# Per-pass denominators by small DMAs instead of transposes, and both context halves transposed in one run

## The chip, the cores and the metric

The kernel runs on one core of a Trainium2 chip. The metric is the device time of one execution in microseconds (us), taken as the median of several executions. The profile is one further execution recorded by the hardware profiler; its own time stands beside the median below.

## The reference

Two graph layers run one after the other on `x` of shape 8 x 2048 x 256 with one adjacency matrix of 2048 x 2048. Layer 0 is a chunked attention with a softmax per chunk of 256 keys. Layer 1, the one that this change touches, is a graph attention with 4 heads of 64:

```python
h = relu(layernorm(x))                      # rows of 256
q = (h @ W).reshape(B, N, 4, 64)
e = e_src[:, :, None, :] + e_dst[:, None, :, :]
e = where(e >= 0, e, 0.2 * e)               # leaky relu
e = where(adj > 0, e, -9e15)
attn = softmax(e, axis=2)                   # over the 2048 sources j
x = x + elu(einsum('bijh,bjhd->bihd', attn, q).reshape(B, N, 256))
```

For each batch `b` and head `h` the kernel needs the weighted sums (the context, 64 numbers for each of 2048 rows) and the softmax denominators (one number for each row). It divides, applies elu, adds `x`, and stores 64 columns of the output.

## The kernel before

Layer 0 fills the first 2730 us or so and is not touched. The second layer is a list of 32 **passes**, one for each of 8 batches and 4 heads (`passes`, L887), of 16 **rounds** each (`rounds`, L888); round `jt` handles 128 sources `j` against all 2048 rows.

The main loop (L901 to L952) writes the instructions of each round by hand, in program order. Every engine takes its own instructions in that order, so an instruction that waits holds up all that stands behind it on its engine. In a round:

- VectorE (DVE) makes the weights `e` two rounds ahead (`clipped`, L804): a max of two factors, clipped by the adjacency limits. There are five `e` buffers, so the weights of round 10 go where those of round 5 were, and wait until every reader of those is done. At the pass's first round ScalarE (ACT) first writes the row factors `near` (L795).
- TensorE (PE) multiplies `e` with the values into two accumulator banks, one for each half of the 64 columns (`weigh_rows`, L815, 8 matmuls a round). Partition 32*blk + d holds column d of row block blk, and the free axis holds the 512 rows of the block.
- For the denominators the rounds go in pairs. ACT scales the even round's weights into two tiles `t` (L926), GpSimd (POOL) adds the odd round's weights to them (L932), and PE sums `t` over the partitions into the bank `den` two rounds later (`add_up_rows`, L826, 4 matmuls). So pair 2, rounds 4 and 5, is summed in round 7. Pairs 3 and 7 (`SINGLE`, L881) skip ACT and POOL and are summed round by round.
- After round 15 ACT copies the accumulators to `cT` (L939) and `den` to `dT` (L948). In `dT` the 512 denominators of block blk fill partition 32*blk and are repeated in the 31 below it.

What is left of a pass is done by a generator, `ending` (L838), during the first rounds of the next pass. `aside` (L194) is a list of generators. `advance` (L213) is called once a round (not in round 13), and resumes each of them once, in order, but stops after one that yields nothing (`None`); one that yields `True` lets the next go on. `ending` stands at the front (L949). Its steps are: load the residual columns `xh` (in round 15); transpose `dT` with four PE transposes and take reciprocals (round 0, yields `None`); transpose the first half of `cT` and multiply (round 1, `None`); the second half (round 2, `None`); then for each half of the rows four ACT operations (L870 to L873, rounds 3 and 5) and two POOL additions (L875, L876, rounds 4 and 6), yielding `True`; then the store (round 7).

Behind it stands `preparation(b + 1)` (L603), which makes the next batch's inputs during a batch's first passes: layer-norm factors on POOL (`roots`, L133 to L136), loads of `x1` (L111), normalisation on ACT (L145), transposes (L157) and copies (L165), small matmuls (L622), and at last eight projections of the values (`sides`, L154, with a DVE product, L693), one for each call of `advance`.

[...]four for `near`, two for the accumulators, and two in the tile `rest`: bank 0 is `den`, bank 1 is what `aux()` returns, used by all transposes and projections.

All loads of the second layer, but those of the first prepared batch, and the stores go through SyncE's queue (SP) in program order: `xh` (L842), the row factors' sources `es` (L594), `x1` (L111), the store (L878).

## Time and profile before

| | |
|---|---|
| median of 3 executions | 4205.73 us (4204.49 to 4206.44) |
| the profiled execution: its own time | 4210.55 us |
| its span, first to last instruction | 4208.7 us |
| granted TensorE clock, mean | 0.994 |
| first `dT` copy (end of pass 0) to the last (end of pass 31) | 2788.8 to 4191.2 us |
| L804, DVE, 128x2048 | 2343 ns, x448 |
| L932, POOL, 128x1024 | 2383 ns, x384 |
| L926, ACT, 128x1024 | 1142 ns, x384 |
| L858, DVE, 128x512 | 681 ns, x64 |
| L157 on `dT`, PE, 128x128 | 273 ns, x128 |

A row of the timeline gives the start, the duration, the engine, the line and operation, what it writes from what, and how many alike in a row; in brackets the idle time of the engine before it and what ended that. Successive instructions of one engine overlap a little [...], so starts are a better measure of pace than durations. Matmul records stand for several instructions on quarters of the array: a round of L815 takes 1.72 us from start to start, a sum of L826 0.86 us, four transposes 0.58 us.

### The profile page before, as it was taken

Reading aid. Unit: us, or ns where it says so; the run is one execution under the profiler, and the core shown is the slowest. Engines: PE = TensorE matmul, PEld = TensorE weight load, DVE = VectorE, ACT = ScalarE, POOL = GpSimd, SP = SyncE. Lnnn points to the kernel's source line nnn. Section 1 sums busy time; section 2 is a strip of 40 time slices with the busy share of each in tenths; the row PEclk is TensorE's granted clock in tenths of the full one; section 3 lists DMA queues with packets and bytes.
Section 4 is the critical chain, followed back from the end, with each engine's and each line's share of the span. In section 5 each row is a group of like instructions: output and inputs, shape, how many; then the busy total and the mean of one; then the engine's idle time right before and its main releaser. Section 6 shows DMA issues by size and latency. Waiting matters only on the chain. (4 is left out here: it accounts for less than half of the span.)

```text
span 4208.7 us, 85702 instructions
## 1 busy us (share of the span) xinstructions
PE 4067.2 (97%) x34998; PEld 1507.0 (36%) x34998; DVE 3159.1 (75%) x3526; ACT 2394.9 (57%) x3090; POOL 3263.0 (78%) x1735
## 2 busy tenths in 40 slices
PE   7999999999999999999999999889999999999998
PEld 3333333333333333333333333333333333333333
DVE  5786676666766677676677677588888988888897
ACT  5655565555565565555556556564555646555554
POOL 2577787888888888788788799777776877777687
PEclk9999999999999999999999999999999999999999
DMA  3221211112112112111211222221221222122121
GB/s 112 87 77 50 57 58 48 53 53 65 48 55 63 48 51 61 54 50 53 62 50 54 55 60 62 80 58 51 63 71 33 72 52 73 51 63 71 33 61 37
DMA packets 343235, 248.11 MB, mean 59 GB/s; under 512 B 225840, under 2 KB 293168, under 8 KB 342832
## 3 DMA queue, kind: packets, MB, share of 16 engines
q1 hardware_dynamic: 337648, 223.66, 19.6%
q0 software_dynamic: 5184, 18.88, 1.2%
q8 instruction: 277, 4.54, 0.4%
q14 instruction: 126, 1.03, 0.1%
HBM read 204.15 MB, written 36.18 MB: 57 GB/s over the span
## 5 line engine op out<-in xcount | busy, mean ns | idle before, releaser
L449 DVE SCALAR_TENSOR_TENSOR E<-big,limit 128x1024 f32<-128x1024 f32 x1024 | 1181.9, 1217 | 646.1 <-PE big L441 627.9
L742 POOL TENSOR_TENSOR add<-E 128x1024 f32<-128x1024 f32 x512 | 1203.7, 2374 | 496.1 <-PE both L461 472.7
L455 ACT ACTIVATE E<-E 128x1024 f32<-128x1024 f32 x1024 | 1055.7, 1057 | 687.8 <-DVE E L449 669.1
L804 DVE SCALAR_TENSOR_TENSOR e<-near,far,limit 128x2048 f32<-128x2048 f32 (+1 forms) x576 | 1183.0, 2107 | 94.3 <-issue 55.0
L932 POOL TENSOR_TENSOR t<-t,e 128x1024 f32<-128x1024 f32 x384 | 903.9, 2383 | 346.4 <-ACT t L926 196.0
L461 PE MATMUL both<-E,v 128*32 128x512 f32 x8192 | 993.9, 594 | 0.2
L815 PE MATMUL acc<-e,qn 128*32 128x512 f32 x8192 | 972.8, 595 | 5.3 <-DVE e L804 5.1
L441 PE MATMUL big<-qT,kT 64*128 64x512 f32 x4096 | 959.4, 606 | 14.6 <-DVE E L449 12.5
L441 PEld LDWEIGHTS big<-qT,kT 64*128 64x128 f32 x4096 | 366.2, 187 | 587.7 <-issue 419.8
L926 ACT ACTIVATE t<-e,quot 128x1024 f32<-128x1024 f32 x384 | 420.1, 1144 | 266.5 <-DVE e L804 153.1
L501 POOL TENSOR_TENSOR acc<-acc,c 128x1024 f32<-128x1024 f32 x224 | 531.2, 2371 | 4.6 <-DVE c L499 4.6
L461 PEld LDWEIGHTS both<-E,v 128*32 128x32 f32 x8192 | 294.3, 109 | 535.8 <-issue 396.7
L815 PEld LDWEIGHTS acc<-e,qn 128*32 128x32 f32 x8192 | 271.8, 110 | 496.0 <-issue 451.4
L499 DVE TENSOR_TENSOR c<-both,r 128x512 f32<-128x512 f32 x448 | 308.7, 690 | 42.3 <-PE both L461 10.6
L472 PE MATMUL big<-add,ones 128*32 128x512 f32 x2048 | 280.7, 601 | 13.9 <-POOL add L742 3.4
L826 PE MATMUL rest<-t,for_sums 128*32 128x512 f32 x1536 | 211.0, 594 | 22.2 <-DVE z L858 9.5
L479 ACT COPY s<-big 128x512 f32<-128x512 f32 x256 | 149.8, 585 | 71.1 <-PE big L472 70.8
L826 PE MATMUL rest<-e,for_sums 128*32 128x512 f32 x1024 | 141.0, 592 | 0.0
L145 ACT ACTIVATE h<-x,off,rstd 128x256 f32<-128x256 f32 x256 | 139.2, 593 | 0.0
L154 PE MATMUL rest<-w,hT 128*32 128x256 f32 x1952 | 122.1, 392 | 10.7 <-DVE qn L693 6.6
L795 ACT ACTIVATE near<-es,off_s 128x1024 f32<-128x1024 f32 x64 | 71.6, 1119 | 106.8 <-DVE e L804 95.8
L154 PE MATMUL big<-hT,wk 128*32 128x512 f32 x1024 | 124.2, 600 | 7.0 <-ACT hT L165 5.8
(133 smaller groups left out, 3031.3 us busy)
## 6 DMA issues: line engine op xcount, KB each, us to landing
r<-inv SPq DMA_DIRECT2D x1024, 64.0 KB
x<-in_x_dram SPq DMA_DIRECT2D x96, 512.0 KB
es<-er SPq DMA_DIRECT2D x64, 512.0 KB
adj_in<-in_adj_dram SPq DMA_DIRECT2D x32, 512.0 KB
x<-o POOLq DMA_DIRECT2D x32, 512.0 KB, 3.3
xh<-x SPq DMA_DIRECT2D x32, 512.0 KB
out_dram<-xh SPq DMA_DIRECT2D x32, 512.0 KB
x<-x SPq DMA_DIRECT2D x28, 512.0 KB
```

Of the source, the lines that this page charges most:

```text
L441: nc.tensor.matmul(ps[:, hh, :], ks[kt // NT][own, hp, (kt % NT) * P : (kt % NT + 1) * P], qs[qb][own, hp, :], start=True, stop=True,)
L449: nc.vector.scalar_tensor_tensor(e, ps, -0.5, bcast(limit[:, qb, kt, :], 1, 2), ALU.max, ALU.min)
L455: nc.scalar.activation(e, e, AF.Exp, scale=0.25 * EDGE)
L461: nc.tensor.matmul(both[part][32 * h : 32 * h + 32, :], vs[kt // NT][:, kt % NT, mine], es[h // 2][:, h % 2, :], start=first, stop=not first,)
L499: nc.vector.tensor_tensor(to[:, part, :], both[part], r, ALU.mult)
L501: nc.gpsimd.tensor_tensor(acc, acc, to, ALU.add)
L742: nc.gpsimd.tensor_tensor(both, tiles[0][hp], tiles[1][hp], ALU.add)
L804: nc.vector.scalar_tensor_tensor(e[:, of, :], near[:, of, :], far[:, jt, h : h + 1], limit[:, of, jt, :], ALU.max, ALU.min,)
L815: nc.tensor.matmul(acc[part][32 * blk : 32 * blk + 32, :], qn[jt // NT][:, jt % NT, own], e[:, blk, :], start=(jt == 0), stop=(jt == NKT - 1),
L826: nc.tensor.matmul(den[32 * blk : 32 * blk + 32, :], for_sums[:, jt, :], blocks[blk], start=first, stop=last,)
L926: nc.scalar.activation(t, now[:, 2 * half : 2 * half + 2, :], AF.Copy, scale=quot[:, m, h : h + 1])
L932: nc.gpsimd.tensor_tensor(ts[half], ts[half], now[:, 2 * half : 2 * half + 2, :], ALU.add)
```

## The change

`dT` is no longer transposed on PE. Four DMAs on SP's queue take the row of 512 denominators at partition 32*blk and lay it over 128 partitions, four numbers in each: partition p gets rows 4p to 4p + 3 of the block. The reciprocal then reads this tile in SBUF. So that the context comes out in the same arrangement, ACT writes `cT` with its columns reordered (it reads PSUM at steps of four), and `xh` and the output are moved by four DMAs each, a block at a time, with four neighbouring rows in a partition. Both halves of `cT` are transposed in one run of eight, the first into `aux()`, the second into bank 0 of `rest`, where `den` will be started in round 3. The reciprocal, the maximum and both products follow at once, and `ending` yields `None` once where it did three times.

```diff
-    def column(to, h):
-
-        return to[:, h * DH : (h + 1) * DH].rearrange("(n p) d -> p n d", p=P)
+    def columns(to, h):
+
+        mine = to[:, h * DH : (h + 1) * DH].rearrange("(b p t) d -> b p t d", b=NQB, t=NT)
+        return [mine[blk] for blk in range(NQB)]
 
     def ending(k, cT, dT):
 
         b, h = passes[k]
         xs = big.tile([P, NKT, DH], F32, tag="acc", name="xh")
-        nc.sync.dma_start(xs, column(x1[b], h))
+        r = small.tile([P, NQB, NT], F32, tag="inverse", name="inverse")
+        for blk in range(NQB):
+            nc.sync.dma_start(r[:, blk, :], dT[32 * blk : 32 * blk + 1, :].rearrange("o (p t) -> o p t", t=NT))
+        for blk, mine in enumerate(columns(x1[b], h)):
+            nc.sync.dma_start(xs[:, NT * blk : NT * blk + NT, :], mine)
         yield True
-        ps = aux().rearrange("p (c k) -> p c k", c=NT)
-        for c in range(NT):
-            flip(ps[:, c, :], dT[:, c * P : (c + 1) * P])
-        r = small.tile([P, NT, NQB], F32, tag="inverse", name="inverse")
-        nc.vector.reciprocal(r, ps.rearrange("p c (b k) -> p c b k", k=32)[:, :, :, 0])
-        nc.vector.tensor_reduce(
-            inverse_most[:, k : k + 1], r.rearrange("p c b -> p (c b)"), mybir.AxisListType.X, ALU.max
-        )
-        yield
+        halves = [aux(), rest[0][:, 0, :]]
+        for part in range(2):
+            for t in range(NT):
+                flip(halves[part][:, t * P : (t + 1) * P], cT[:, part, t, :])
         z = big.tile([P, NQB, NT, DH], F32, tag="c", name="z")
+
+        nc.vector.reciprocal(r, r)
+        nc.vector.tensor_reduce(inverse_most[:, k : k + 1], r, mybir.AxisListType.XY, ALU.max)
         for part in range(2):
-            ps = aux().rearrange("p (t f) -> p t f", t=NT)
-            for t in range(NT):
-                flip(ps[:, t, :], cT[:, part, t * P : (t + 1) * P])
             nc.vector.tensor_tensor(
                 z[:, :, :, 32 * part : 32 * part + 32].rearrange("p b t d -> p t b d"),
-                ps.rearrange("p t (b d) -> p t b d", d=32),
-                bcast(r, 3, 32),
+                halves[part].rearrange("p (t b d) -> p t b d", t=NT, d=32),
+                bcast(r.rearrange("p b t -> p t b"), 3, 32),
                 ALU.mult,
             )
-            yield
+        yield
         low = big.tile([P, NQB, NT, DH], F32, tag="c", name="low")
...
-        nc.sync.dma_start(column(out[b], h), xs)
+        for blk, mine in enumerate(columns(out[b], h)):
+            nc.sync.dma_start(mine, xs[:, NT * blk : NT * blk + NT, :])
...
-            cT = big.tile([P, 2, QB], F32, tag="hT", name="cT", bufs=1)
+            cT = big.tile([P, 2, NT, P], F32, tag="hT", name="cT", bufs=1)
             for part in range(2):
-                nc.scalar.copy(cT[:, part, :], acc[part])
+                nc.scalar.copy(cT[:, part, :, :], acc[part].rearrange("p (k t) -> p t k", t=NT))
```

## The prediction

> **What bounds the kernel now.** I read the page's busy times first. They don't settle it: PE stands at 97% over the whole span, but the change touches the second layer alone.

> ```profile
> PE 4067.2 (97%) x34998; PEld 1507.0 (36%) x34998; DVE 3159.1 (75%) x3526; ACT 2394.9 (57%) x3090; POOL 3263.0 (78%) x1735
> ```

> So I cut that layer at the dT copies (L948), pass by pass. From pass 4 on the lengths repeat every four passes; 28 to 31 prepare no batch. The rows are passes 4, 5, 6, 7 and 29: stretch, length, then busy us of PE, PEld, DVE, ACT, POOL.

> ```profile
> 2927.64:2974.28 46.64, 44.00 (x396) 14.35 (x392) 41.69 (x25) 29.14 (x42) 36.93 (x20) 1.00 0.36 102
> 2974.28:3017.05 42.77, 42.13 (x400) 14.56 (x404) 36.57 (x24) 27.14 (x39) 33.23 (x16) 1.00 0.22 51
> 3017.05:3069.97 52.92, 51.52 (x576) 19.26 (x568) 44.93 (x34) 22.68 (x32) 33.82 (x19) 1.00 0.10 25
> 3069.97:3111.30 41.33, 40.42 (x382) 14.88 (x384) 36.33 (x23) 21.89 (x27) 33.28 (x16) 1.00 0.24 70
> 4069.86:4110.29 40.43, 39.11 (x350) 13.94 (x348) 38.00 (x23) 21.89 (x26) 33.29 (x16) 1.00 0.21 59
> ```

> Nothing there has room: PE idles 0.6 to 2.6 us a pass, and in pass 29 DVE idles only the 2.4 us in which ACT rewrites `near`. The order inside a pass must decide, so the last view is the timeline of a plain pass, 30.

> ```profile
> 4110.29 0.58 ACT L948 COPY dT<-rest 128x512 f32<-128x512 f32 x1 [1.13 <-PE rest L826]
> ...
> 4112.97 4.73 POOL L932 TENSOR_TENSOR t<-t,e 128x1024 f32<-128x1024 f32 x2 [6.31 <-DVE e L804]
> 4114.97 0.25 DVE L848 RECIPROCAL inverse<-rest 128x16 f32<-128x16 f32 x1
> ...
> 4117.85 4.70 POOL L932 TENSOR_TENSOR t<-t,e 128x1024 f32<-128x1024 f32 x2 [0.15 <-DVE e L804]
> ...
> 4121.17 0.63 ACT L870 ACTIVATE low<-z 128x512 f32<-128x512 f32 x1 [3.89 <-DVE z L858]
> ...
> 4123.06 1.28 POOL L875 TENSOR_TENSOR z<-z,low 128x512 f32<-128x512 f32 x1 [0.51 <-ACT z L872]
> ...
> 4125.67 4.73 POOL L932 TENSOR_TENSOR t<-t,e 128x1024 f32<-128x1024 f32 x2
> ...
> 4130.37 1.28 POOL L875 TENSOR_TENSOR z<-z,low 128x512 f32<-128x512 f32 x1
> 4130.72 1.07 PE L826 MATMUL rest<-t,for_sums 128*32 128x512 f32 x8
> ```

> Let T0 be the start of the dT copy, 4110.29. POOL hardly rests: pairs 0 and 1 of its additions, half 0 of the ending (2.61 us from start to start), pair 2, then half 1. Pair 2 ends at 4130.40; PE sums that pair at 4130.72, T0 + 20.43. From there PE never waits until the pass ends: 2 sums, 8 rounds and 5 sums are 7 x 0.86 + 8 x 1.72 = 19.8, with 0.27 before the copy 40.5, against 40.43 measured. So pair 2 on POOL is already just in time.

> **The change, part by part.**

> *Removed from PE:* four dT transposes, 0.58 us a pass, and the waits at the three former steps (in pass 30: 0.33 for the reciprocal, 0.55 and 0.43 for the products). At most 1.9 us a pass, 61 in all, if PE had nothing else to wait for. Eight transposes of cT stay; DVE's four operations stay.

> *The denominators' DMAs.* The nearest row is layer 0's small copy of sums, also to 128 pieces: SP and DVE in the timeline,

> ```profile
> 2365.23 0.54 SPq L481 DMA_DIRECT2D sum<-s  x1
> ...
> 2367.08 0.25 DVE L486 RECIPROCAL sum<-sum 128x16 f32<-128x16 f32 x1
> ```

> 1.85 us from issue to use, 1.92 the median of 112 such waits, 3.85 the longest. Four issues at 0.54 + 0.05 put the last one 1.77 after the first, so r is there at T0 + 0.58 + 0.03 + 1.77 + 1.92 = T0 + 4.3. [...] The row of r<-inv has four issues in 1.69 us, none waiting for the one before, so I take 4.3[...].

> *What waits behind it.* DVE's reciprocal used to start at T0 + 4.68, when the weights of round 2 were done; those will be early by about a microsecond, so DVE stalls up to 1 us, with round 3's weights behind it. Then reciprocal 0.28, maximum 0.09, products 0.60 and 0.68: z at T0 + 6.0, where it was at 10.8. The second product stands ahead of round 3's weights, which PE reaches early and awaits; cover: PE's savings.

> *The order on POOL, which I think decides.* The ending now yields None once, so its halves move two rounds forward: half 0 goes ahead of pair 1, half 1 ahead of pair 2. POOL's total is the same, but pair 2 is now behind 2.61 us more. In a plain pass: ACT's L870 to L872 end at T0 + 7.8; POOL's half 0 runs 7.9 to 10.5, pair 1 to 15.2, half 1 to 17.8, pair 2 to 22.5 instead of 20.1. PE's sum of pair 2 waits for its second tile until 22.6; then 0.43 + 0.86 + 8 x 1.72 + 5 x 0.86 + 0.27 = 19.6, so the next T0 is at 42.2: **+1.75 us**. Late next: pair 2 reads e of round 5, whose buffer round 10 needs, so DVE stalls about 1 us too, inside the same delay. With r at once, POOL would still need 2.7 + 3 x 4.72 + 2 x 2.61 = 22.1; better DMAs alone don't cure it.

> *With a preparation.* Pass 4: the layer-norm factors (POOL 3.9 us from 2939.98 to 2943.87) come ahead of half 0 as well; pair 2 ends at T0 + 25.5 where it was 23.5. Loads of x1 now stand on SP behind r, xh (about 1 us of wire each, by xh's 4 us) and es (4.5 us the pair), landing about T0 + 16, and ACT's normalisation waits for them, holding the pair copies. PE has 19.6 and about 4.5 of transposes and waits left: 49.6 against 46.64, **+3.0**. Pass 5: the same chain with less left to lose, about 44.0, **+1.2**. Pass 6: PE-bound; it gains a projection (1.72) which no longer spills into pass 7, loses 0.58 and 1.2 of waits: **0**. Pass 7: loses that projection and its 0.69 wait, and becomes a plain pass of 42.2 to 42.8: **+1.2**. Per batch +5.4.

> *The cT copies* read PSUM at steps of 16 bytes. [...] No row here has such a step; the nearest (L939 itself, and L165, runs of 128) take 0.585 us. Doubled to 1.17 [...], the second would end at T0 - 0.2, before dT can start: nothing. Tripled, dT starts about 1 us late in each pass, +32. I take nothing. *xh and the store* in four DMAs: three more issues each of about 0.45 on an idle SP; xh lands by T0 + 8 for half 0, when needed. At the very end the last store has only half the data left to move, about -2, against +1 for r.

> **Sum:** 7 batches x 5.4 = 37.8; passes 28 to 31 4 x 1.75 = 7.0; passes 1 to 3 (138.9 us before, with the same steps) 4.4; tail -1: **+48** on the profiled 4210.55 (span 4208.7). The median lies 4.8 below that execution; a difference carries over: 4205.7 + 48 = **4254**.

> **Rivals.**

> *Faster (4180).* PE is the bound in passes 5 to 7 and takes its 0.58 and waits. Place: the sum of pair 2. If POOL ended that pair by T0 + 20.1 as now, the removed work would be worth about 1 us in 24 passes. For: PE at 97%. Against: the 22.1 just worked out without any DMA. It would take POOL 2 us off that stretch.

> *No change (4206).* The DMA is hidden and POOL's delay eats just the savings. For: pass 6.

> *Late denominators (4310).* If r needs the longest wait seen, 3.85, all passes but the fourth kind lengthen by nearly the extra 1.9: +55 to +60 more. For: DVE stands right behind it. Against: the queue is empty then. [...]

> *A slow cT copy or loads in the way (4290).* As above, +32 to +40 more.

> **How the numbers follow.** Chances: the forecast 0.68, late denominators 0.12, slow copy or loads 0.06, no change 0.05, faster 0.09. 0.2% (8.4 us) is about what a measurement of this kernel can tell. Faster 0.09, same 0.05, slower 0.86. The forecast's own range is 4235 to 4275 (r between 1 us sooner and 0.7 later). With no change and most of the late cases inside, 4206 to 4308 leaves out the faster case and about 0.08 above.

> **What would show it.** Right: plain passes of about 42.2 us; the reciprocal waiting up to 1 us for a DMA; PE waiting some 2 us for POOL at the sum of pair 2; POOL's order half 0, pair 1, half 1, pair 2; pass 4 near 49.6. Wrong: plain passes at or under 40.4, pair 2 ending before T0 + 20.5, a reciprocal released more than 5 us after T0, or cT copies well over 0.6 us.

## The result, and the profile after

The changed kernel takes **4262.82 us** (median; 4260.52 to 4264.04) against 4205.11 for the kernel before beside it: ratio **1.0139**, 95% interval 1.0123 to 1.0155. It is 58 us slower; the forecast was 4254, with 4206 to 4308 around it. The profiled execution took 4260.52 us, its span is 4258.6.

The page's busy line has hardly moved, PE's share least of all. From it alone one would not guess a loss of 58 us:

```profile
PE 4069.7 (96%) x34870; PEld 1477.8 (35%) x34870; DVE 3161.3 (74%) x3526; ACT 2394.3 (56%) x3090; POOL 3262.7 (77%) x1735
```

PE has 128 matmuls fewer and the same busy time. The second layer, cut at the dT copies (now L949) as before, shows where the time is. The rows are passes 4, 5, 6, 7 and 30, in the columns of the prediction's table (the second column from the right is the DMA share, the third the granted clock):

```profile
2924.60:2973.47 48.87, 44.53 (x396) 14.19 (x388) 40.09 (x24) 31.38 (x46) 36.90 (x20) 1.00 0.31 87
2973.47:3018.32 44.85, 42.52 (x392) 13.93 (x396) 37.86 (x28) 25.80 (x38) 33.79 (x19) 0.96 0.23 53
3018.32:3071.56 53.24, 51.30 (x602) 19.78 (x596) 41.87 (x30) 21.91 (x28) 33.27 (x16) 1.00 0.15 41
3071.56:3114.79 43.23, 40.11 (x352) 12.39 (x352) 40.05 (x24) 21.86 (x26) 33.29 (x16) 1.00 0.20 50
4154.00:4196.90 42.90, 39.23 (x348) 12.29 (x344) 38.19 (x23) 21.84 (x26) 33.28 (x16) 1.00 0.18 50
```

Every stretch is longer, and PE idles 1.9 to 4.3 us where it idled 0.6 to 2.6. The clock is no longer 1.00 everywhere; the last section comes back to that. A plain pass, 30, as rows of the timeline; T0 is 4154.00:

```profile
4154.00 0.59 ACT L949 COPY dT<-rest 128x512 f32<-128x512 f32 x1 [1.13 <-PE rest L826]
4154.61 2.46 SPq L845 DMA_DIRECT2D inverse<-dT  x4
4156.23 4.69 POOL L933 TENSOR_TENSOR t<-t,e 128x1024 f32<-128x1024 f32 x2 [7.32 <-ACT t L927]
4158.68 0.25 DVE L855 RECIPROCAL inverse<-inverse 128x16 f32<-128x16 f32 x1 [1.53 <-DMA inverse<-dT]
...
4160.37 0.63 ACT L870 ACTIVATE low<-z 128x512 f32<-128x512 f32 x1 [3.18 <-DVE z L858]
4162.26 1.28 POOL L875 TENSOR_TENSOR z<-z,low 128x512 f32<-128x512 f32 x1 [1.34 <-ACT z L872]
4162.65 1.92 PE L815 MATMUL acc<-e,qn 128*32 128x512 f32 x16 [2.39 <-DVE e L804]
4164.87 4.73 POOL L933 TENSOR_TENSOR t<-t,e 128x1024 f32<-128x1024 f32 x2
4169.55 1.29 POOL L875 TENSOR_TENSOR z<-z,low 128x512 f32<-128x512 f32 x1
4172.16 14.21 POOL L933 TENSOR_TENSOR t<-t,e 128x1024 f32<-128x1024 f32 x6
...
4176.92 0.62 PE L826 MATMUL rest<-t,for_sums 128*32 128x512 f32 x2 [1.26 <-POOL t L933]
```

POOL's order is the program's: half 0 (4162.26), pair 1 (4164.87), half 1 (4169.55), pair 2 (4172.16), each begun when the one ahead had ended, to within 0.1 us. PE gets pair 2's second tile at T0 + 22.92, after a wait for POOL; before, it summed the whole pair at T0 + 20.43. From there to the next dT copy it takes 19.98 us, about what it took before (20.00). The earlier wait of 2.39 us for `e` at 4162.65 is the DVE's stall of 1.53 for the DMA with the products behind it: 2.39 us that the pass doesn't feel, since PE has to wait for pair 2 anyway.

All passes together, in us from the first dT copy to the last (kinds are means over the six batches in passes 4 to 27):

| | first copy at | passes 1–3 | pass 4 | 5 | 6 | 7 | plain | last copy to end | first copy to last |
|---|---|---|---|---|---|---|---|---|---|
| before | 2788.8 | 138.9 | 46.62 | 42.77 | 52.91 | 41.33 | 40.43 | 17.5 | 1402.4 |
| after | 2781.3 | 143.3 | 48.88 | 44.83 | 53.57 | 43.34 | 42.88 | 18.8 | 1458.5 |

The layer is 56.1 us longer and the end 1.3: 57.4, which is the difference of the medians, 57.7. The two profiled executions differ by only 50.0, because that of the kernel before lost 7.4 us ahead of the first copy; the last section has that.

### The profile page after: what moved, and what is told of

It reads as the page before. It is cut to its first block, busy times and chain, and to the rows that moved or that the text cites. A ratio compares the mean times of both kernels' runs of the same rounds, so it can differ in the third digit from the quotient of the medians.

```text
span 4258.6 us, 86046 instructions
## 1 busy us (share of the span) xinstructions
PE 4069.7 (96%) x34870; PEld 1477.8 (35%) x34870; DVE 3161.3 (74%) x3526; ACT 2394.3 (56%) x3090; POOL 3262.7 (77%) x1735
## 3 DMA queue, kind: packets, MB, share of 16 engines
q14 instruction: 131, 1.07, 0.1%
## 4 chain that ended last, share of the span: by engine, by line
PE 73%; POOL 8%; ACT 6%; DVE 4%; DMA 3%; issue 3%; SPq 2%; POOLq 0%; ACTq 0%; DVEq 0%
PE big L441 17%; PE both L461 16%; PE acc L815 14%; PE big L154 9%; PE big L472 6%; PE rest L826 6%; POOL add L742 3%; PE rest L154 3%; POOL acc L501 2%; POOL t L933 2%; ACT E L455 2%; DMA inverse<-dT 1%; SPq L845 1%; DVE e L804 1%; PE big L157 1%
## 5 line engine op out<-in xcount | busy, mean ns | idle before, releaser
L804 DVE SCALAR_TENSOR_TENSOR e<-near,far,limit 128x2048 f32<-128x2048 f32 (+1 forms) x576 | 1178.6, 2105 | 115.5 <-issue 78.9
L815 PE MATMUL acc<-e,qn 128*32 128x512 f32 x8192 | 1035.3, 602 | 42.2 <-DVE e L804 41.9
L826 PE MATMUL rest<-t,for_sums 128*32 128x512 f32 x1536 | 257.8, 606 | 18.4 <-POOL t L933 12.9
L826 PE MATMUL rest<-e,for_sums 128*32 128x512 f32 x1024 | 172.2, 593 | 0.0
L154 PE MATMUL rest<-w,hT 128*32 128x256 f32 x1952 | 118.3, 383 | 18.3 <-DVE z L858 13.5
L154 PE MATMUL big<-hT,wk 128*32 128x512 f32 x1024 | 124.9, 603 | 6.8 <-ACT hT L165 5.8
L472 PEld LDWEIGHTS big<-add,ones 128*32 128x32 f32 x2048 | 49.1, 107 | 224.4 <-issue 141.2
```

The costliest lines, as they stand in the source:

```text
L154: nc.tensor.matmul(to[j : j + 32], lhsT[:, j : j + 32], rhs, start=start, stop=stop)
L472: nc.tensor.matmul(sums[32 * h : 32 * h + 32, :], ones, es[h // 2][:, h % 2, :], start=True, stop=True)
L804: nc.vector.scalar_tensor_tensor(e[:, of, :], near[:, of, :], far[:, jt, h : h + 1], limit[:, of, jt, :], ALU.max, ALU.min,)
L815: nc.tensor.matmul(acc[part][32 * blk : 32 * blk + 32, :], qn[jt // NT][:, jt % NT, own], e[:, blk, :], start=(jt == 0), stop=(jt == NKT - 1),
L826: nc.tensor.matmul(den[32 * blk : 32 * blk + 32, :], for_sums[:, jt, :], blocks[blk], start=first, stop=last,)
```

## The experiments

Three causes could account for the 58 us. **P**, the forecast: the halves of the ending stand two rounds earlier in POOL's order, so that half 1 holds up pair 2. **D**: DVE's wait for the four DMAs holds up the weights. **S**: the additional issues on SP hold up the loads of the next batch's preparation. All edits below are against the changed kernel, but for the one that says otherwise.

**1. POOL's order back, the DMA wait kept.** Two bare yields after the products send both halves of the ending two rounds back; preparation starts in round 3 again.

```diff
         yield
+        yield
+        yield
         low = big.tile([P, NQB, NT, DH], F32, tag="c", name="low")
```

> The changed kernel with the ending yielding None three times again, all of them after the products, so that both halves go back to rounds 3 to 6 on ACT and POOL; DMAs for the denominators, the run of eight transposes and the four-part loads stay. Theory P (the order on POOL decides: half 1 ahead of pair 2 delays PE's sum of pair 2): pair 2 ends near T0 + 20 again, plain passes (28 to 31) fall from 42.9 to 40.4 to 40.7 us although DVE still waits for the denominators, whole time 4212 to 4225. Theory D (the wait of the reciprocal for its DMA decides, since DVE has no idle time in a plain pass but near's): the 1.5 us wait stays in every pass, plain passes 41.9 or more, 4245 to 4262. Theory S (loads queue up on SP behind the many small DMAs): passes 4 and 5 stay at 48.9 and 44.8.

Measured: 4238.32 us, ratio 1.0085 (1.0069 to 1.0100). Plain passes 40.72 to 41.43, pass kinds 49.30, 43.14, 54.10, 41.71. The plain passes recover four fifths of what they had lost (40.96 in the mean, from 42.88), with the DMAs still there, so there it is P and not D. Passes of the kinds of 5 and 7 recover about as large a part (43.14 from 44.83, 41.71 from 43.34). But those of the kinds of 4 and 6 recover nothing and are even 0.4 and 0.5 us longer: 4238 is a miss against the expectation, and the order on POOL can't be all. Pass 12 (of the kind of pass 4, T0 = 3299.65) shows what is left:

```profile
3304.21 0.25 DVE L855 RECIPROCAL inverse<-inverse 128x16 f32<-128x16 f32 x1 [0.19 <-DMA inverse<-dT]
...
3308.18 1.92 PE L815 MATMUL acc<-e,qn 128*32 128x512 f32 x16 [2.11 <-DVE e L804]
3308.30 4.73 POOL L935 TENSOR_TENSOR t<-t,e 128x1024 f32<-128x1024 f32 x2 [1.64 <-DVE e L804]
...
3324.28 6.87 DVE L804 SCALAR_TENSOR_TENSOR e<-near,far,limit 128x2048 f32<-128x2048 f32 x3 [2.60 <-POOL t L935]
...
3324.30 1.07 PE L826 MATMUL rest<-t,for_sums 128*32 128x512 f32 x2 [1.25 <-POOL t L935]
```

The reciprocal waits 0.19 us only (in the other five passes of this kind 0.29 to 1.37). It is the work itself that is late: reciprocal, maximum and products stand ahead of round 3's weights, so pair 1 waits on POOL for `e` (1.64), with the layer-norm factors, half 0 and pair 2 behind it. A second order, DVE's.

**2. The same, with the preparation let go at once.**

```diff
         yield
+        yield True
+        yield True
         low = big.tile([P, NQB, NT, DH], F32, tag="c", name="low")
```

> As the one before, but the two added steps yield True, so that the halves go back to rounds 3 to 6 while the preparation still runs from round 1 as in the changed kernel. Theory P: plain passes 40.4 to 40.7; only passes with a preparation keep a loss, pass 4 at 49 to 50 (the factors of the layer norm stand ahead of pair 1 on POOL), whole time 4225 to 4240. Theory D: as before, plain 41.9 or more, 4245 to 4262.

Measured: 4224.97, ratio 1.0051 (1.0035 to 1.0066); plain 40.71 to 40.92, kinds 48.00, 42.59, 53.39, 41.28. I had expected it above the first run; it is 13 us below, with passes of the kind of 4 at 48.0 in the mean, where 49 to 50 was expected. Letting the preparation start in round 1 is not what makes the changed kernel slow. A plain pass from here, T0 = 4119.16:

```profile
4123.82 0.25 DVE L855 RECIPROCAL inverse<-inverse 128x16 f32<-128x16 f32 x1 [0.26 <-DMA inverse<-dT]
...
4127.79 1.92 PE L815 MATMUL acc<-e,qn 128*32 128x512 f32 x16 [2.19 <-DVE e L804]
...
4135.22 4.72 POOL L935 TENSOR_TENSOR t<-t,e 128x1024 f32<-128x1024 f32 x2
```

PE still loses 2.19 us to the late `e`, but pair 2 starts at T0 + 16.06 and ends at 20.8, and the pass is within 0.5 us of before.

**3. No DMA, the new order kept.** The denominators come through PE transposes again, in the same step, with the new arrangement of the rows.

```diff
-        for blk in range(NQB):
-            nc.sync.dma_start(r[:, blk, :], dT[32 * blk : 32 * blk + 1, :].rearrange("o (p t) -> o p t", t=NT))
...
+        for t in range(NT):
+            flip(halves[0][:, t * P : (t + 1) * P], dT[:, t, :])
+        nc.vector.reciprocal(
+            r.rearrange("p b t -> p t b"),
+            halves[0].rearrange("p (t b k) -> p t b k", t=NT, k=32)[:, :, :, 0],
+        )
...
-        nc.vector.reciprocal(r, r)
...
-            dT = const.tile([P, QB], F32, tag="wk", name="dT")
-            nc.scalar.copy(dT, den)
+            dT = const.tile([P, NT, P], F32, tag="wk", name="dT")
+            nc.scalar.copy(dT, den.rearrange("p (k t) -> p t k", t=NT))
```

> The changed kernel with the denominators' DMAs undone: dT is copied in the new order and transposed by four PE transposes as before, everything else as in the changed kernel (both halves in one run, one None). No DMA is waited for by the reciprocal. Theory P: POOL's order is unchanged, so plain passes stay at 42.3 to 43 and the whole at 4250 to 4270, no faster than the changed kernel by more than 10 us. Theory D: the 2.4 us a pass are gone, plain passes 40.4 to 40.7, 4205 to 4215.

Measured: 4260.22, ratio 1.0138 (1.0123 to 1.0154): nothing regained. Plain passes 42.33 to 42.35. Pass 30, T0 = 4153.80:

```profile
4156.87 0.25 DVE L850 RECIPROCAL inverse<-rest 128x16 f32<-128x16 f32 x1
...
4170.17 1.28 POOL L879 TENSOR_TENSOR xh<-xh,z 128x512 f32<-128x512 f32 x1
...
4171.41 7.03 POOL L936 TENSOR_TENSOR t<-t,e 128x1024 f32<-128x1024 f32 x3
...
4176.15 0.62 PE L826 MATMUL rest<-t,for_sums 128*32 128x512 f32 x2 [1.26 <-POOL t L936]
```

The reciprocal doesn't wait for a transfer and comes at T0 + 3.07 where it came at 4.68. Pair 2 still stands behind half 1, and its second tile is there at T0 + 22.35 instead of 22.92. **D falls**: of the 2.44 us that a plain pass lost, the DMAs account for 0.5, the place on POOL for the rest. Passes of the kinds of 4, 5 and 6 are 0.04, 0.5 and 0.4 us shorter than in the changed kernel. In those of the kind of 7 the PE transposes take that back: those of cT write the bank that DVE reads the denominators from, and PE waits for it, 2.18 us in pass 7, which is 44.3 us long. (The reciprocal of such a pass waits for no DMA in the changed kernel either, but for 0.46 us in one of six.)

**4. Both orders back, DMAs and one run of transposes kept.** Reciprocal and products one round later, halves in rounds 3 and 5 as before.

```diff
                 flip(halves[part][:, t * P : (t + 1) * P], cT[:, part, t, :])
+        yield
         z = big.tile([P, NQB, NT, DH], F32, tag="c", name="z")
...
         yield
+        yield
         low = big.tile([P, NQB, NT, DH], F32, tag="c", name="low")
```

> The changed kernel with the eight transposes in round 0, reciprocal and products in round 1, and the halves from round 3 as before (three Nones, one of them between transposes and reciprocal). Round 3's weights stand ahead of the reciprocal, which gives the DMA 2.3 us more, and POOL has its old order. Theories P and D agree: plain passes 40.4, no wait for the DMA over 0.2 us, and PE's four transposes and waits come off the passes where PE is the bound (5 and 6, by 0.3 to 1 us each): 4190 to 4207. Theory S: passes 4 and 5 stay above 48 and 44, 4225 or more.

Measured: 4200.77, ratio 0.9995 (0.9986 to 1.0003): **the whole loss is gone**, with all the DMAs still in place. Kinds 46.77, 42.49, 52.89, 40.97, plain 40.43. So S falls too: pass 4 is at its old length with the same issues on SP ahead of the loads. A plain pass, first its windows row, then rows of its timeline (T0 = 4096.37):

```profile
4096.37:4136.81 40.44, 38.80 (x346) 11.33 (x344) 38.01 (x23) 21.90 (x27) 33.23 (x16) 1.00 0.19 53
```

```profile
4099.40 9.39 POOL L935 TENSOR_TENSOR t<-t,e 128x1024 f32<-128x1024 f32 x4 [6.73 <-DVE e L804]
...
4103.66 0.24 DVE L856 RECIPROCAL inverse<-inverse 128x16 f32<-128x16 f32 x1
...
4103.80 1.92 PE L815 MATMUL acc<-e,qn 128*32 128x512 f32 x16 [0.27 <-DVE e L804]
...
4107.62 1.92 PE L815 MATMUL acc<-e,qn 128*32 128x512 f32 x16 [1.04 <-DVE e L804]
...
4109.88 1.92 PE L815 MATMUL acc<-e,qn 128*32 128x512 f32 x16 [0.34 <-DVE e L804]
```

The reciprocal now stands behind round 3's weights, the DMAs are in by then (not in passes of the kind of 5, where it still waits 1.1 to 1.5 us and the pass is none the longer), and pairs 0 and 1 run back to back. It also shows what the removed transposes are worth: the pass is 40.44, as before. PE is idle 1.6 us, waiting for `e`: DVE is busy 38.01, and the 2.39 us in which ACT rewrites `near` make 40.40. Where PE was given room, DVE is the bound. Over the layer the gain is 1402.4 − 1397.5 = 4.9 us, and the end takes 1.3 of that back.

**5. POOL's order new, DVE's old.** The converse of the first two: the products behind round 3's weights, half 0 in the same step.

```diff
                 flip(halves[part][:, t * P : (t + 1) * P], cT[:, part, t, :])
+        yield
         z = big.tile([P, NQB, NT, DH], F32, tag="c", name="z")
...
-        yield
         low = big.tile([P, NQB, NT, DH], F32, tag="c", name="low")
```

> The changed kernel with the transposes in round 0 and the reciprocal, the products and the first ACT step together in round 1. Round 3's weights stand ahead of the products on DVE, as in the kernel before, while POOL keeps the changed order: half 0 ahead of pair 1, half 1 ahead of pair 2. Theory P (the order on POOL suffices): the halves start some 2.3 us later still, pair 2 ends near T0 + 25, plain passes 44 to 45 us, 4280 to 4330. Theory Q (the products ahead of round 3's weights on DVE do it, POOL's order matters little by itself): plain passes 40.4 to 41, 4200 to 4215.

Measured: 4295.16, ratio 1.0216 (1.0200 to 1.0231), plain 43.48 to 43.54. Pass 30, T0 = 4184.76:

```profile
4190.09 0.24 DVE L856 RECIPROCAL inverse<-inverse 128x16 f32<-128x16 f32 x1
...
4203.52 7.04 POOL L933 TENSOR_TENSOR t<-t,e 128x1024 f32<-128x1024 f32 x3
...
4208.27 0.62 PE L826 MATMUL rest<-t,for_sums 128*32 128x512 f32 x2 [1.26 <-POOL t L933]
```

No wait for the DMA, weights that PE awaits for 0.44 us at most, and the largest loss of all, though below the 44 to 45 us expected of a plain pass: z is later, so half 0 and half 1 are, and pair 2 behind them reaches PE at T0 + 23.51. POOL's order alone does it.

**6. As run 4, with the preparation let go from round 1.**

```diff
                 flip(halves[part][:, t * P : (t + 1) * P], cT[:, part, t, :])
+        yield
         z = big.tile([P, NQB, NT, DH], F32, tag="c", name="z")
...
-        yield
+        yield True
+        yield True
         low = big.tile([P, NQB, NT, DH], F32, tag="c", name="low")
```

> As the kernel with the products a round later and the halves from round 3, but only the transposes' step yields None; the two others yield True, so that the preparation may run in rounds 1 and 2. If the preparation's place is worth what the two spread kernels differ by (13 us), 4180 to 4192, faster than both kernels; the plain passes stay at 40.4. If that difference came from the early products only, 4197 to 4204, no gain over the kernel before.

Measured: 4228.65, ratio 1.0056 (1.0042 to 1.0069): a miss, 25 us above the higher of the two ranges and 37 above the lower. Passes 5 and 7 are shorter (41.17, 40.43), as hoped, but pass 6 is at 56.2 us. Its windows row, of the first batch:

```profile
3013.85:3069.58 55.73, 52.93 (x602) 19.19 (x596) 41.87 (x30) 22.03 (x27) 33.22 (x16) 0.97 0.15 39
```

All eight projections are in it now (602 matmuls against 576 in the kernel before), ahead of the first of them PE waits 2.8 us for the products, which must empty the bank that the projections want, and part of it runs at a lower clock.

**7. The kernel before with the preparation let go.** Against the kernel before; the three bare yields become `yield True`.

```diff
-        yield
+        yield True
         z = big.tile([P, NQB, NT, DH], F32, tag="c", name="z")
...
-            yield
+            yield True
         low = big.tile([P, NQB, NT, DH], F32, tag="c", name="low")
```

> The kernel before, its three transposing steps yielding True instead of None, so that the preparation runs beside them; nothing else of the change. If freeing the preparation is what can be gained here, with or without the change: 4188 to 4200. If the single aux bank makes PE wait for each read in turn, so that it takes the change's second bank: 4203 to 4225, passes 4 to 6 longer and plain passes still 40.4.

Measured: 4234.65, ratio 1.0068 (1.0053 to 1.0083), 10 us above the higher range. Pass 5 grows from 42.8 to 48.6 (it takes over projections of pass 6: 472 matmuls where it had 400), pass 6 gets 51.7 and pass 7 40.1:

```profile
2980.88:3029.44 48.56, 46.03 (x472) 16.30 (x464) 41.20 (x31) 25.86 (x38) 33.80 (x19) 1.00 0.22 49
```

So an early preparation is no gain of its own. It moves the same work from pass to pass: here it costs 3.9 us a batch against the kernel before, in run 6 it cost 2.4 against run 4, and in run 2 it gained 3.0 against run 1. (The clock also fell, eight times in run 6 and ten in run 1, against none in run 4 and four in run 2; what that cost wasn't separated.)

**8. One bare yield and nothing else.** Transposes in round 0, products in round 1, half 0 in rounds 2 (ACT) and 3 (POOL), half 1 in rounds 4 and 5. On POOL half 0 stands behind pair 1, half 1 behind pair 2: the old order.

```diff
                 flip(halves[part][:, t * P : (t + 1) * P], cT[:, part, t, :])
+        yield
         z = big.tile([P, NQB, NT, DH], F32, tag="c", name="z")
```

> The changed kernel with one bare yield put ahead of the reciprocal and the products, and nothing else: transposes and DMAs in round 0, reciprocal and products in round 1, the two halves in rounds 2 and 3, so that POOL's order is that of the kernel before (half 0 before pair 2, half 1 after it) and VectorE's products stand after round 3's weights. Theory of orders (POOL's in all passes, VectorE's in the passes with preparation): the plain passes are 40.4 us again, as they are in the run with products a round later; passes 4, 5 and 7 within 0.5 us of that run's 46.8, 42.5 and 41.0 and pass 6 within 1.5 us of 52.9: 4195 to 4212 us in all. Theory that the spacing of the halves matters too (half 1 one round behind half 0 and not two): plain passes 40.6 to 41.5, 4210 to 4235. Theory that the DMA wait decides: plain passes stay above 42, 4250 to 4265.

Measured: 4213.92, ratio 1.0024 (1.0016 to 1.0031), 2 us above the range of the theory of orders. Plain passes 40.43, exactly as expected. POOL in pass 30 (T0 = 4116.49) has pairs 0 and 1, half 0, pair 2, half 1:

```profile
4119.52 9.37 POOL L934 TENSOR_TENSOR t<-t,e 128x1024 f32<-128x1024 f32 x4 [6.74 <-DVE e L804]
4128.86 1.27 POOL L876 TENSOR_TENSOR z<-z,low 128x512 f32<-128x512 f32 x1
...
4131.45 4.71 POOL L934 TENSOR_TENSOR t<-t,e 128x1024 f32<-128x1024 f32 x2
4136.12 1.29 POOL L876 TENSOR_TENSOR z<-z,low 128x512 f32<-128x512 f32 x1
```

The theory of the spacing is not tested by this, against what the expectation says: each half takes two rounds, and half 1 starts 7.26 us behind half 0 on POOL, as in the kernel before (7.31). Pass 4 at 47.01 fits. Pass 5 doesn't (44.51 against 42.5 expected): in the first of them PE waits 1.88 us for the preparation's logs and 0.96 for its transposed rows. Pass 7 is a microsecond shorter than expected (39.96), since its last projection has gone into pass 6.

| run | POOL: half 1 | DVE: products | DMA for r | preparation from round | plain pass | kinds 4 to 7, sum | ratio |
|---|---|---|---|---|---|---|---|
| before | after pair 2 | after round 3's weights | no | 3 | 40.43 | 183.6 | 1 |
| after | before pair 2 | before them | yes | 1 | 42.88 | 190.6 | 1.0139 |
| 3 | before | before | no | 1 | 42.34 | 190.8 | 1.0138 |
| 5 | before | after | yes | 1 | 43.51 | 194.7 | 1.0216 |
| 1 | after | before | yes | 3 | 40.7–41.4 | 188.3 | 1.0085 |
| 2 | after | before | yes | 1 | 40.7–40.9 | 185.3 | 1.0051 |
| 4 | after | after | yes | 3 | 40.43 | 183.1 | 0.9995 |
| 8 | after | after | yes | 2 | 40.43 | 184.8 | 1.0024 |
| 6 | after | after | yes | 1 | 40.43 | 185.6 | 1.0056 |

None is clearly faster than the kernel before. Run 4 keeps all of the change but its timing, and is equal to it.

## Why the prediction was right

**The sum came to 48, the measurement to 58.** One slip made it look better than it was: it counts 7 batches where passes 4 to 27 are 6. Its own terms give 6 × 5.4 + 7.0 + 4.4 − 1 = 42.8. The mechanism held and the terms were too small, by 14.6 in all: 2.8 in the plain passes, 9.5 in passes 4 to 27, 2.3 at the end. Passes 1 to 3 came out as forecast, 4.4.

**The order on POOL, "which I think decides".** Right, shown from both sides: runs 3 and 5 keep the new order and keep the loss; run 4 undoes it and the loss is gone, run 8 undoes it and 9 of the 58 us are left. Step by step in the plain pass, predicted and measured in us after T0: half 0 on POOL at 7.9 and 8.26, pair 1 done at 15.2 and 15.6, half 1 done at 17.8 and 18.16, pair 2's second tile at 22.6 and 22.92. The estimate of 22.1 with r at once was 22.35 in run 3. The pass was to be +1.75 and is +2.44. Two terms were short: r (below) by 0.4, and the remainder after pair 2, 19.6 against 19.98, by 0.4.

**The denominators' DMAs.** Predicted at T0 + 4.3, measured at 4.68: the four issues took 2.46 us (0.6 each), 0.1 more than reckoned, but the last took about 2.2 us to arrive where the median in layer 0 was 1.92. From the first issue to use the four are 4.07 us, where four such waits of 1.92 in a row would have made 7.7 (an estimate from that median): they do overlap, which the prediction took from the four issues of `r<-inv` in 1.69 us alone. The stall of DVE, "up to 1 us", was 1.53. Late denominators as a rival would have needed passes of 44.

**What the removed transposes are worth.** "At most 1.9 us a pass if PE had nothing else to wait for" was rightly kept out of the sum, but for a reason that was not seen in full. The rival *Faster* took them for about 1 us in 24 passes if only pair 2 came in time. In run 4 it does, and a plain pass gains nothing: DVE's 38.0 and the 2.4 for `near` make 40.4. The prediction named those two numbers and didn't add them. The 24 passes 4 to 27 gain 3 us together in run 4, 0.5 a batch.

**The second order.** The prediction saw that the products would stand ahead of round 3's weights, and covered that with PE's savings. In the plain passes this held. In passes with a preparation it failed: run 1 keeps only that order and is 37.5 us above run 4, which undoes it too. Not all of it is the order: in pass 12 pair 2 is 0.9 us later than in run 4 (T0 + 24.64 against 23.72), and PE takes 24.5 us from there instead of 23.1, with its clock at half rate for 3.4 of them (in the row shown there the two matmuls take 1.07 us, in run 4 0.62). In pass 20 of run 1 the clock fell earlier, where PE had to wait for pair 2 anyway: from pair 2 on PE takes 23.05 us, as in run 4, and the order by itself costs 1.0. How the 37.5 us divide in all wasn't measured.

**With a preparation.** Pass 4 was to be +3.0 and is +2.26. Pair 2 was to end at T0 + 25.5, and in pass 12 its second tile is summed at 25.5; PE had 23.4 left, not 24.1. The loads did land late, as said (ACT waits 1.44 us for `x` there), but between half 1 and the pair copies, where it costs nothing. Pass 5 was to be +1.2 by "the same chain" and is +2.06. The chain is another: PE waits for ACT's normalised `h`, which now stands behind half 0's four ACT instructions. In the three of its kind without a fall of the clock it is +1.4. Pass 6: 0 predicted, +0.66 measured; pass 7: +1.2 and +2.01. It did lose its projection (352 matmuls where it had 382) and did become a plain pass, but a plain pass was 0.7 us more than the 42.2 thought.

**The cT copies, and the end.** The strided copies take 0.585 us in the median of 64, as the contiguous ones did: reading at 16-byte steps cost ACT nothing here. That it might double or triple the copies was the author's estimate, with no row behind it, and so was the 2 us at the last store. The end was to gain 1 us and lost 1.3. The store's issue, before and after:

```profile
4203.28 0.38 SPq L878 DMA_DIRECT2D out_dram<-xh  x1
```

```profile
4250.73 3.90 SPq L879 DMA_DIRECT2D out_dram<-xh  x4
```

From the end of POOL's last addition to the end of the span it is 5.4 us in both: having half the data left to move bought nothing, and the 1.3 is r, which z waits for.

## What to carry to other kernels

When a step is split or joined, write down for each in-order engine which of its instructions now stand ahead of which, before counting what the change saves: here 2.6 us of POOL work in front of the wrong pair of tiles cost 2 us in each plain pass, and the DMAs themselves half a microsecond. Place the consumer of a small transfer behind work that is due anyway: with one yield more (run 8) the reciprocal waited for no DMA in a plain pass, where it had waited 1.5 us. And before pricing the relief of an engine at 97%, add up the next engine's busy time and its fixed wait in that same stage: here 38.0 and 2.4 us came to the 40.4 of the pass.

## What the runs showed of the hardware

```profile
2982.70 0.93 PE L157 MATMUL rest<-ident,h 128*128 128x128 f32 x4 [1.64 <-ACT h L145]
2983.56 3.26 PE L815 MATMUL acc<-e,qn 128*32 128x512 f32 x16
```

```profile
3366.04 0.93 PE L157 MATMUL rest<-ident,h 128*128 128x128 f32 x4 [1.72 <-ACT h L145]
3366.90 1.92 PE L815 MATMUL acc<-e,qn 128*32 128x512 f32 x16
```

Nearly the same wait, and once a round of 3.26 us and once one of 1.92. In each of the ten profiles all falls begin on one grid of steps of 3.41 us: their distances are whole multiples of it, to 1 ns. Here are the steps that hold the two waits, each with the one after it:

```profile
2980.59:2984.00 3.41, 1.72 (x16) 0.56 (x12) 3.41 (x2) 3.41 (x6) 3.05 (x3) 1.00 0.93 291
2984.00:2987.41 3.41, 3.41 (x20) 0.83 (x16) 3.41 (x3) 3.38 (x7) 3.41 (x3) 0.50 0.43 114
...
3362.88:3366.29 3.41, 1.69 (x18) 0.44 (x10) 3.41 (x3) 3.10 (x6) 3.05 (x2) 1.00 0.93 250
3366.29:3369.71 3.42, 3.01 (x28) 0.81 (x26) 3.42 (x2) 3.42 (x6) 3.34 (x3) 1.00 0.49 166
```

PE was busy for half of either step. That is just where it goes both ways. Of the full-clock steps in passes 1 to 31 of all ten profiles, 44 have PE idle for 1.95 us or more, and every one is followed by a step at half the clock; of 47 with 1.68 to 1.94 us idle, 7 are; of some 4000 with less, none. So in these profiles the falls go with the idle time within one step, not with the length of a single wait. In pass 12 of run 1 the waits of 1.50 and 1.25 us, neither long by itself, fall mostly into one step, with 1.14 us of work left in it, and the next step is at 0.50:

```profile
3320.41:3323.83 3.42, 1.14 (x8) 0.14 (x4) 1.26 (x1) 0.00 (x0) 3.42 (x2) 1.00 0.34 77
```

Runs 4, 7 and 8, whose longest PE wait is 1.9 us, have no fall in passes 1 to 31; the changed kernel has 10, run 1 10, runs 2 and 3 four each, run 5 15 and run 6 eight.

What a fall costs depends on the place: in passes 29 and 31 PE had to wait for pair 2 anyway, and they are as long as passes 28 and 30 (42.79 to 42.95). Where PE is the bound it counts: comparing passes of one kind with and without it, three of pass 5's kind, one of pass 6's and one of pass 7's are together about 6 us longer. In four of these five the reciprocal also came 0.4 to 1.0 us later than in the others of their kind, so that only the 0.65 us of pass 5 can be put down to the clock alone. That is about 6 of the 58 at most, and no step of the prediction had it. It wasn't tried by itself.

**The same at the change of layers.** In the profiled execution of the kernel before, PE waited 3.25 us ahead of the first of five early projections (L154), and three of them took 3.64 us each; after, the wait was 1.52 and all took 1.93 or 1.94. Windows from 2704 to 2722, before and after:

```profile
2704.00:2722.00 18.00, 13.07 (x136) 5.46 (x132) 3.91 (x7) 2.77 (x3) 10.41 (x8) 0.65 0.77 246
```

```profile
2704.00:2722.00 18.00, 12.15 (x196) 5.83 (x188) 5.60 (x9) 2.78 (x3) 9.24 (x7) 1.00 0.74 246
```

The granted clock in these 18 us is 0.65 before and 1.00 after. The two waits and the three projections differ by 1.7 + 3 × 1.7 = 6.8 us, out of the 7.4 us by which the first dT copy came later before than after, and so most of what the two profiled executions understate of the difference of the medians. The profiles of runs 7 and 8 have the late first copy too (2788.7 and 2788.2), those of the other six runs do not (2779.5 to 2784.6). What made that one wait longer stays open.
